# A gather ring with 24 more places, and a tile order of its own, for the last of four graph layers

## The chip, the cores and the metric

The kernel runs on one core of one Trainium2 chip. The metric is the device time of one execution in microseconds (us); less is better. The engines of the core are named as the profile names them: PE multiplies matrices, DVE works element by element, ACT evaluates functions, POOL (GpSimd) here mostly issues indirect DMAs and multiplies, and SP issues plain DMAs. PEld is PE's loading of weights.

## What is computed

Four layers of graph attention, each on a layer-normalised input and added to it. Eight batches of 2048 nodes with 64 features share one adjacency matrix, which is sparse: a node has about four neighbours on average, and the first ones have by far the most. The change concerns the fourth layer:

```python
def _layernorm(x, axis=-1, eps=1e-5):
    m = jnp.mean(x, axis=axis, keepdims=True)
    v = jnp.var(x, axis=axis, keepdims=True)
    return (x - m) / jnp.sqrt(v + eps)

def _L3_gnn_ref(x, adj, W, a):
    h = jnp.matmul(x, W)
    f1 = jnp.einsum('bnf,f->bn', h, a[:F_out, 0])
    f2 = jnp.einsum('bnf,f->bn', h, a[F_out:, 0])
    e = jax.nn.leaky_relu(f1[:, :, None] + f2[:, None, :], negative_slope=0.2)
    e = jnp.where(adj[None, :, :] > 0, e, NEG_BIG)
    attention = jax.nn.softmax(e, axis=2)
    return jax.nn.relu(jnp.matmul(attention, h))

# --- layer 3 (adj_preln) ---
h = jnp.maximum(_layernorm(x, axis=-1), 0.0)
x = x + _L3_gnn_ref(h, adj, L3_gnn_W, L3_gnn_a)
```

The other three layers are of the same kind: layer 1 has the same additive scores, layers 0 and 2 use dot products.

## The kernel before

**Tiles and slots.** The 2048 nodes are 16 tiles of 128, one node per partition; a row holds all eight batches, 512 features (`F`), and in the additive layers 8 further numbers (`B`), one score per batch. Each tile has a fixed number of slots, `ROWS[i]` plain ones and `PACKED[i]` packed ones: tile 0 has 9 + 8 = 17, tile 1 has 8, tile 2 has 6, tiles 3 to 5 have 5, tiles 6 to 10 have 4, and tiles 11 to 15 have 3; 81 in all. A slot is one gathered row for each of the 128 partitions. In a plain slot the neighbour belongs to the partition's own node. A packed slot holds the neighbours of nodes that have too many, and matrices of zeros and ones (`sel`, `selt`) carry values between node and slot through PE.

**The ring.** `gather` (L246) issues one indirect DMA on POOL for each slot of a tile, from the layer's table in HBM (2048 rows of 520 numbers) into the next place of `ring`, a buffer of `RING = 26` places. `held[i]` is the place at which tile i begins and `front` the next place to be filled. A place may be filled again only when the tile that was in it has been used up, in `weigh_sum`. The ring is shared by all layers.

**A layer as a pipeline.** `pipeline` (L214) takes stages and issues them in turn: in step n, each stage s works on the tile `order[n - s]`, the later stages first. What the engines run follows these program orders closely, though the framework may move an instruction by its own estimate of times. For layer 3, `additive(4, wd3, relu_add)` has these stages:

- `take` gathers the tile's rows.
- `sums` (L504) takes the exponentials of the rows' scores (ACT, L507) and adds them over a node's slots (`by_query`, PE, L399), for a bound of the softmax.
- `first` (L522) carries the node's own score to the packed slots (`by_edge`, PE, L412), adds, applies the leaky function, and takes the exponential (ACT, L542): the weights.
- `check` (L547) is `second`: sums of weights, and `weigh_sum` (L372), which multiplies two slots at a time by their weights on DVE (L380, `wg`) and adds them up in PSUM by a matmul with the identity or `selt` for each slot (PE, L385, `y`). After it the places of the tile are free. Beside it `xs_rows` loads the tile's `x` on SP (L259, six buffers).
- `third` (L553) divides on DVE (L465, `att`), transposes on PE (L306) and copies on ACT (L307, `xt`).
- `project` (L558) multiplies by the layer's matrix (PE, L561, `q`), and `relu_add` (L905) applies the relu, adds `x` on DVE (L906) and stores the result on SP (L907).

**What goes before.** The pipeline of layer 2's second half ends with `pre_d`, which computes the scores for layer 3 and stores `xh` into table 4; after the last tile it stores a mean row as well (`mr`, L366). Every gather of layer 3 needs the whole table, so layer 3 begins when that row has landed. Both pipelines take their working buffers from one pool, `rows2`, and use `ORDER`: tiles 13, 12, 11, 10, 9, 8, 0, 7, 6, 1, 5, 2, 4, 3, 14, 15.

Of the kernel before, what the change touches and what calls it, by code (L numbers as in the profile page):

```python
# [1 line left out]

# [6 lines left out]
F32 = mybir.dt.float32  # L9
# [7 lines left out]
P = 128  # L17
# [12 lines left out]
PACKED = [8, 2, 3, 3, 2, 1, 2, 1, 1, 1, 1, 2, 2, 1, 1, 1]  # L30
WIDTH = [128, 24, 24, 24] + [16] * 12
SEGS = [(24, 2), (16, 1)] + [(8, 1)] * 14
RING = 26
TEMP = 16.0

PAIRS = [0, 0, 2, 2, 2, 0, 0, 0, 2, 2, 2, 2, 2, 2, 2, 2]
# [4 lines left out]
ORDER1 = [13, 14, 15, 12, 11, 10, 0, 7, 6, 1, 5, 2, 4, 3, 9, 8]  # L41
ORDER2 = [8, 9, 10, 12, 11, 13, 0, 7, 6, 1, 5, 2, 4, 3, 14, 15]
ORDER = [13, 12, 11, 10, 9, 8, 0, 7, 6, 1, 5, 2, 4, 3, 14, 15]


def segments(n, count, least):
# [13 lines left out]
def edge_stack(ctx: ExitStack, tc: tile.TileContext, x_in, adj, w1, w1t, a1, wh, wht, bh, wo, bo,  # L60
# [10 lines left out]
    N, F = x_in.shape  # L71
    D = gamma.shape[0]
    B = F // D
# [3 lines left out]
    SLOTS = [k + t for k, t in zip(ROWS, PACKED)]  # L77
# [20 lines left out]
    most = const.tile([P, 5, NT], F32, name="most")  # L98
    least = const.tile([P, 2, NT], F32, name="least")
    ring = const.tile([P, RING, F + B], F32, name="g")  # L100
    qidx = const.tile([P, sum(PACKED)], I32, name="qidx")
# [5 lines left out]
    table = [tc.dram_tile([N + 2, F + B if k in (1, 4) else F], F32, name=f"table{k}")  # L107
             for k in range(5)]
# [9 lines left out]
    sel_all = [None]  # L118
# [93 lines left out]
    order = list(MAKING)  # L212
# [10 lines left out]
    bank, spot, rows_pool, more_pool, own_pool, thin = [None], [0], [None], [None], [None], [None]  # L223
# [7 lines left out]

    held, front = {}, [0]

    def rows(i, lo, hi, most=RING):

        t = lo
        while t < hi:
            at = (held[i] + t) % RING
            m = min(most, hi - t, RING - at)
            yield t, m, ring[:, at:at + m, :]  # L240
            t += m

    def row(i, t):
        return ring[:, (held[i] + t) % RING, :F]

    def gather(k, i, st):  # L246

        n = SLOTS[i]
        assert sum(SLOTS[j] for j in held) + n <= RING
        held[i], front[0] = front[0], (front[0] + n) % RING  # L250
        cols = table[k].shape[1]
        for t in range(n):
            nc.gpsimd.indirect_dma_start(  # L253
                out=ring[:, (held[i] + t) % RING, :cols], out_offset=None, in_=table[k][:, :],
                in_offset=bass.IndirectOffsetOnAxis(ap=idx[:, OFF[i] + t:OFF[i] + t + 1], axis=0))

    def load(st, name, src, bufs):
# [134 lines left out]
    def by_query(i, w, cols):  # L392


        K, T = ROWS[i], PACKED[i]
        w, packed = w if isinstance(w, list) else (w[:, :K, :], w[:, K:, :])
        p = (thin[0] or ps_m).tile([P, F], F32, name="m")
        for t in range(T):
            nc.tensor.matmul(p[:, :cols], selt(i, t), packed[:, t, :], start=(t == 0), stop=(t == T - 1))  # L399
        if K == 1:  # L400
            return w[:, 0, :], p[:, :cols]
        d = small.tile([P, cols], F32, name=f"row{cols}")
        nc.vector.tensor_reduce(d, w.rearrange("p k c -> p c k"), AX.X, OP.add)
        return d, p[:, :cols]
# [10 lines left out]
    def scores(i, st, q):  # L415

        K, s = ROWS[i], slots(s_all, i)
        qp = ps_q.tile([P, F], F32, name="q")
        nc.scalar.copy(qp, q)
        for t0, m, g in rows(i, 0, K, 2):  # L420
            pr = rows_pool[0].tile([P, 2, F], F32, name="prod")
            nc.vector.tensor_tensor(pr[:, :m], qp[:, None, :].to_broadcast([P, m, F]), g[:, :, :F],  # L422
                                    op=OP.mult)
            nc.vector.tensor_reduce(s[:, t0:t0 + m, :], pr[:, :m].rearrange("p t (b d) -> p t b d", b=B),
                                    AX.X, OP.add)
        for t in range(K, SLOTS[i]):
            qe = ps_q.tile([P, F], F32, name="q")
            nc.tensor.matmul(qe, sel(i, t - K), q, start=True, stop=True)  # L428
            pr = rows_pool[0].tile([P, 2, F], F32, name="prod")
            nc.vector.tensor_tensor(pr[:, 0], qe, row(i, t), op=OP.mult)  # L430
            nc.vector.tensor_reduce(s[:, t, :], heads(pr[:, 0]), AX.X, OP.add)
        return s
# [67 lines left out]
    def additive(k, wd, *finish):  # L500
# [213 lines left out]
    with tc.tile_pool(name="l2", bufs=2) as l2p, \  # L714
# [29 lines left out]
        def score(i, st, lo, hi):  # L744

            K, n = ROWS[i], hi - lo
            w = l2p.tile([P, max(ROWS), B * H], F32, name="w2", bufs=5)[:, :n]
            st.setdefault("w", []).append(w)
            s = ps_s.tile([P, F], F32, name="s2")[:, :n * B * H].rearrange("p (t c) -> p t c", c=B * H)
            for t in range(lo, hi):  # L750
                q = st["q"] if t < K else sent[i, t - K]
                g = ps_g.tile([P, F], F32, name="g2")
                nc.scalar.copy(g, row(i, t))  # L753
                pr = l2p.tile([P, B * H, D], F32, name="prod2")
                nc.vector.tensor_tensor(  # L755
                    pr.rearrange("p (b h) d -> p b h d", h=H),
                    q[:, :B * H * D].rearrange("p (b h d) -> p b h d", h=H, d=D),
                    heads(g)[:, :, None, :].to_broadcast([P, B, H, D]), op=OP.mult)
                nc.vector.tensor_reduce(s[:, t - lo, :], pr, AX.X, OP.add)  # L759
                nc.vector.tensor_tensor(s[:, t - lo, :], s[:, t - lo, :], q[:, B * H * D:], op=OP.subtract)  # L760
                nc.scalar.activation(w[:, t - lo], s[:, t - lo], AF.Exp, bias=mbb[:, OFF[i] + t:OFF[i] + t + 1])  # L761
                if t >= K:
                    fetch(stream.index((i, t - K)) + QE)
# [85 lines left out]
        thin[0] = None  # L849
    own.close()  # L850

    with psum_pools()[0] as ps_q, psum_pools()[1] as ps_t, tc.tile_pool(name="rows2", bufs=2) as rp:
        rows_pool[0] = rp
        order[:] = ORDER
        bank[0] = ps_t.tile([P, F], F32, name="tiny")
        sel_all[0] = rp.tile([P, sum(PACKED) * P], F32, name="sel", bufs=1)
        nc.sync.dma_start(out=sel_all[0], in_=sel_dram[:, :])

        def take3(i, st):
# [42 lines left out]
        pipeline(take3, first3, second3, third3, both(pre_b, xs_rows), fourth3, pre_b, pre_c(u3), pre_d(4, u3))  # L902


        def relu_add(i, st):  # L905
            nc.vector.scalar_tensor_tensor(st["x"], st["p"], 0.0, st["x"], op0=OP.max, op1=OP.add)  # L906
            nc.sync.dma_start(out=out[i * P:(i + 1) * P, :], in_=st["x"])  # L907

        additive(4, wd3, relu_add)


        nc.vector.memset(most[:, 3, :], 0.0)
# [527 lines left out]
```

## Time and profile before

| what | us |
|---|---|
| median of 3 runs | 1720.55 |
| lowest and highest | 1719.27, 1725.79 |
| the profiled execution | 1721.51 |
| its span, first to last instruction | 1719.7 |
| layer 3, from the issue of the mean row to the end | 1526.9 to 1719.7 |
| first and last gather of layer 3 begin | 1529.04 and 1670.20 |
| last store of layer 3 is issued | 1714.9 |

An instruction's row in the timeline gives its start and duration in us, the engine, the source line, the operation, the output and inputs by their names in the program, and in brackets how long the engine had been idle before it and what it then waited for. "issue" is a wait for nothing that the profile shows, and "remote" one for which it finds no source. Ends of matmuls are modelled. The view by stretches gives the busy time of each engine between two moments, then PE's granted clock as a share of the full one, the share of time in which the DMA engines were busy, and the bytes per second.

### The profile page before, as it was taken

To read this page: it belongs to the slowest core of one execution; us is meant where nothing else is said; L and a number is where in the kernel's file an instruction comes from. 1 tells how busy PE (TensorE), PEld (TensorE's weight loads), DVE (VectorE), ACT (ScalarE), POOL (GpSimd) and SP (SyncE) were. 2 spreads that over 40 slices of the span, in tenths; PEclk is the share of its full clock that TensorE was granted. 3 is DMA by queue.
4 is the path that set the end of the run, shared out by engine and by line. 5 is a ranking of instruction groups with operands and counts; after the bars stand their busy time and mean duration, and the time that the engine had idled before them with its cause. 6 is when DMAs were issued, how large, how long until landed. Compare 5 with 4: busy or idle time off the path is not lost.

```text
span 1719.7 us, 15784 instructions
## 1 busy us (share of the span) xinstructions
PE 1215.1 (71%) x3771; PEld 606.6 (35%) x3771; DVE 1318.4 (77%) x2748; ACT 744.5 (43%) x2378; POOL 1153.4 (67%) x903
## 2 busy tenths in 40 slices
PE   0025667776479974599997999999467877555877
PEld 0002334443234431234342444443223433333545
DVE  6979999992469987699997899831389889823656
ACT  5841324441146783356531545545234445620011
POOL 5766867786554125898789889985577896654540
PEclk9998876896699997799999999999787879657989
DMA  5555454455566447656255345200643542235651
GB/s 172 167 182 179 152 200 153 141 198 156 147 201 235 158 179 260 233 189 208 87 201 200 113 157 177 87 13 19 255 141 99 154 146 70 81 119 164 197 170 51
DMA packets 85787, 266.94 MB, mean 155 GB/s; under 512 B 14627, under 2 KB 14659, under 8 KB 75446
## 3 DMA queue, kind: packets, MB, share of 16 engines
q0 software_dynamic: 37328, 141.05, 26.7%
q1 hardware_dynamic: 48358, 124.79, 20.4%
q8 instruction: 32, 0.52, 0.1%
q14 instruction: 69, 0.57, 0.1%
HBM read 208.74 MB, written 57.05 MB: 155 GB/s over the span
## 4 chain that ended last, share of the span: by engine, by line
PE 25%; POOL 11%; DVE 9%; issue 7%; ACT 5%; DMA 3%; another core or an unknown queue 2%; DVEq 0%; SPq 0%; POOLq 0%; ACTq 0%
PE y L787 10%; PE y L385 4%; POOL g L253 3%; POOL wh L772 3%; PE m L836 2%; ACT yn L795 2%; PE m L824 2%; PE y L779 2%; POOL wg L380 1%; DMA g<-table,idx 1%; POOL ln_r L290 1%; DMA rows<-table 1%; PE m L399 1%; DVE prod L755 1%
## 5 line engine op out<-in xcount | busy, mean ns | idle before, releaser
L253 POOL DMA_INDIRECT g<-table,idx x405 | 399.2, 986 | 233.5 <-issue 161.7
L772 POOL TENSOR_TENSOR wh<-g,w 128x1024 f32<-128x1024 f32 x162 | 307.5, 1918 | 30.0 <-PE y L787 28.0
L385 PE MATMUL y<-wg,ident 128*128 128x512 f32 x392 | 234.5, 729 | 72.7 <-POOL wg L380 64.3
L290 POOL TENSOR_TENSOR ln_r<-ln_q,mhalf 128x8 f32<-128x8 f32 x80 | 135.8, 1701 | 160.6 <-DVE ln_q L288 85.1
L759 DVE TENSOR_REDUCE s<-prod 128x32 f32<-128x2048 f32 x81 | 184.0, 2286 | 14.8 <-ACT w L761 12.9
L380 POOL TENSOR_TENSOR wg<-g,w 128x1024 f32<-128x1024 f32 (+1 forms) x91 | 158.9, 1756 | 37.3 <-ACT w L436 24.2
L787 PE MATMUL y<-wh,ident 128*128 128x512 f32 x320 | 154.6, 610 | 28.9 <-POOL wh L785 25.1
L385 PE MATMUL y<-wg,selt 128*128 128x512 f32 x256 | 141.6, 663 | 5.4 <-POOL wg L380 4.4
L385 PEld LDWEIGHTS y<-wg,ident 128*128 128x128 f32 x392 | 81.6, 228 | 162.2 <-POOL wg L380 78.9
L787 PE MATMUL y<-wh,selt 128*128 128x512 f32 x256 | 124.7, 614 | 10.4 <-POOL wh L772 10.4
L795 ACT ACTIVATE yn<-y,rec 128x64 f32<-128x64 f32 x512 | 111.2, 368 | 27.5 <-PE y L787 26.9
L755 DVE TENSOR_TENSOR prod<-q,g 128x2048 f32<-128x2048 f32 x49 | 111.5, 2276 | 5.3 <-ACT g L753 4.6
L399 PE MATMUL m<-w,selt 128*128 128x8 f32 (+1 forms) x384 | 59.5, 258 | 76.0 <-ACT w L542 38.2
L380 DVE TENSOR_TENSOR wg<-g,tiny 128x1024 f32<-128x1024 f32 (+1 forms) x92 | 98.2, 1086 | 17.1 <-PE y L385 8.8
L399 PEld LDWEIGHTS m<-w,selt 128*128 128x128 f32 x384 | 63.5, 213 | 122.3 <-ACT w L542 43.6
L442 DVE SCALAR_TENSOR_TENSOR zt<-m,bhc,att 128x512 f32<-128x512 f32 x64 | 47.3, 738 | 75.0 <-ACT att L441 74.4
L298 ACT ACTIVATE xh<-x,ln_r 128x64 f32<-128x64 f32 x256 | 88.3, 428 | 18.8 <-POOL ln_r L292 18.7
L787 PEld LDWEIGHTS y<-wh,ident 128*128 128x128 f32 x320 | 59.0, 193 | 104.9 <-issue 63.8
L428 PE MATMUL q<-rows,sel 128*128 128x512 f32 x128 | 84.3, 762 | 15.7 <-DVE prod L422 5.0
L753 ACT COPY g<-g 128x512 f32<-128x512 f32 x81 | 50.4, 622 | 100.5 <-DVE prod L755 87.9
L755 DVE TENSOR_TENSOR prod<-qe,g 128x2048 f32<-128x2048 f32 x32 | 73.0, 2282 | 17.0 <-DMA qe<-qtab,qidx 15.9
L779 PE MATMUL y<-rows,ident 128*128 128x512 f32 x128 | 70.0, 634 | 18.3 <-DMA rows<-table 13.6
(210 smaller groups left out, 2584.7 us busy)
## 6 DMA issues: line engine op xcount, KB each, us to landing
qtab<-q SPq DMA_DIRECT2D x16, 1040.0 KB
a<-in_adj_dram SPq DMA_DIRECT2D x16, 1024.0 KB
q<-qtab SPq DMA_DIRECT2D x14, 1040.0 KB
table<-xh SPq DMA_DIRECT2D x48, 256.0 KB
rows<-table SPq DMA_DIRECT2D x48, 256.0 KB
xs<-x SPq DMA_DIRECT2D x48, 256.0 KB
x<-xs SPq DMA_DIRECT2D x48, 256.0 KB
table<-xh SPq DMA_DIRECT2D x32, 260.0 KB
```

The costliest lines, as they stand in the source:

```text
L253: nc.gpsimd.indirect_dma_start(out=ring[:, (held[i] + t) % RING, :cols], out_offset=None, in_=table[k][:, :], in_offset=bass.IndirectOffse ...
L290: nc.gpsimd.tensor_tensor(st["rstd"][:, 0, :], q, mhalf, op=OP.pow)
L298: nc.scalar.activation(dst[:, b * D:(b + 1) * D], st["src"][:, b * D:(b + 1) * D], func, bias=0.0 if st["less"] is None else r[:, 1, b:b + ...
L380: eng.tensor_tensor(wg[:, :m].rearrange("p t (b d) -> p t b d", b=B), g[:, :, :F].rearrange("p t (b d) -> p t b d", b=B), w[:, t0:t0 + m, ...
L385: nc.tensor.matmul(y, lhs(i, t), wg[:, t - t0, :], start=(t == 0 and own is None), stop=(t == n - 1))
L399: nc.tensor.matmul(p[:, :cols], selt(i, t), packed[:, t, :], start=(t == 0), stop=(t == T - 1))
L755: nc.vector.tensor_tensor(pr.rearrange("p (b h) d -> p b h d", h=H), q[:, :B * H * D].rearrange("p (b h d) -> p b h d", h=H, d=D), heads(g ...
L759: nc.vector.tensor_reduce(s[:, t - lo, :], pr, AX.X, OP.add)
L772: nc.gpsimd.tensor_tensor(wg, heads(row(i, t))[:, :, None, :].to_broadcast([P, B, 2, D]), w[:, :, 2 * k:2 * k + 2, None].to_broadcast([P, ...
L779: nc.tensor.matmul(st["ys"][j], ident, xb[:, 4 * j:4 * j + 4], start=True, stop=False)
L787: nc.tensor.matmul(st["ys"][j], lhs(i, t), wg[:, 4 * j:4 * j + 4], start=False, stop=(t == n - 1))
L795: nc.scalar.activation(yn[:, b, h, :], st["ys"][j][:, b, h, :], AF.Copy, scale=st["rec"][:, 4 * j + b, 2 * k + h:2 * k + h + 1])
```

## The change

Layer 3 gets a second ring buffer, `gmore`, of `MORE = 24` places behind the 26; `place` tells in which of the two a place lies, and `rows` cuts a tile where one ends. The fill point is set back to 0. The pool `rows2` is closed when layer 2's pipeline has been issued and a new one, `rows3`, is opened in its space, in which `gmore` is the first tile; `sel` moves to a pool `tail` around both. Layer 3 has its own order, `ORDER3`, in which tile 0 is ninth rather than seventh and tile 5 comes ahead of tile 1.

```diff
+MORE = 24
+ORDER3 = [13, 12, 11, 10, 9, 8, 7, 6, 0, 5, 1, 2, 4, 3, 14, 15]
@@ ring
+    rings, room = [ring], [RING]
+
+    def place(at):
+
+        return (rings[0], at, RING - at) if at < RING else (rings[1], at - RING, room[0] - at)
+
     def rows(i, lo, hi, most=RING):
 
         t = lo
         while t < hi:
-            at = (held[i] + t) % RING
-            m = min(most, hi - t, RING - at)
-            yield t, m, ring[:, at:at + m, :]
+            part, at, left = place((held[i] + t) % room[0])
+            m = min(most, hi - t, left)
+            yield t, m, part[:, at:at + m, :]
             t += m
@@ gather
-        assert sum(SLOTS[j] for j in held) + n <= RING
-        held[i], front[0] = front[0], (front[0] + n) % RING
+        assert sum(SLOTS[j] for j in held) + n <= room[0]
+        held[i], front[0] = front[0], (front[0] + n) % room[0]
         cols = table[k].shape[1]
         for t in range(n):
+            part, at, _ = place((held[i] + t) % room[0])
             nc.gpsimd.indirect_dma_start(
-                out=ring[:, (held[i] + t) % RING, :cols], out_offset=None, in_=table[k][:, :],
+                out=part[:, at, :cols], out_offset=None, in_=table[k][:, :],
@@ layer 2, second half, and layer 3
-    with psum_pools()[0] as ps_q, psum_pools()[1] as ps_t, tc.tile_pool(name="rows2", bufs=2) as rp:
-        rows_pool[0] = rp
+    with psum_pools()[0] as ps_q, psum_pools()[1] as ps_t, tc.tile_pool(name="tail", bufs=2) as tail:
+        layer = ExitStack()
+        rows_pool[0] = layer.enter_context(tc.tile_pool(name="rows2", bufs=2))
         order[:] = ORDER
         bank[0] = ps_t.tile([P, F], F32, name="tiny")
-        sel_all[0] = rp.tile([P, sum(PACKED) * P], F32, name="sel", bufs=1)
+        sel_all[0] = tail.tile([P, sum(PACKED) * P], F32, name="sel", bufs=1)
...
         pipeline(take3, first3, second3, third3, both(pre_b, xs_rows), fourth3, pre_b, pre_c(u3), pre_d(4, u3))
 
+        layer.close()
+        rows_pool[0] = layer.enter_context(tc.tile_pool(name="rows3", bufs=2))
+        order[:] = ORDER3
+        rings.append(rows_pool[0].tile([P, MORE, F + B], F32, name="gmore", bufs=1))
+        room[0], front[0] = RING + MORE, 0
...
         additive(4, wd3, relu_add)
+
+        layer.close()
```

More of the change, by code (lines that the diff above doesn't have):

```diff
@@ L1 @@
-from contextlib import ExitStack
+from contextlib import ExitStack, nullcontext
 import concourse.bass as bass
@@ L237, in rows @@
         while t < hi:
-            at = (held[i] + t) % RING
-            m = min(most, hi - t, RING - at)
-            yield t, m, ring[:, at:at + m, :]
+            part, at, left = place((held[i] + t) % room[0])
+            m = min(most, hi - t, left)
+            yield t, m, part[:, at:at + m, :]
             t += m
     def row(i, t):
-        return ring[:, (held[i] + t) % RING, :F]
+        part, at, _ = place((held[i] + t) % room[0])
+        return part[:, at, :F]
     def gather(k, i, st):
         n = SLOTS[i]
-        assert sum(SLOTS[j] for j in held) + n <= RING
-        held[i], front[0] = front[0], (front[0] + n) % RING
+        assert sum(SLOTS[j] for j in held) + n <= room[0]
+        held[i], front[0] = front[0], (front[0] + n) % room[0]
         cols = table[k].shape[1]
         for t in range(n):
+            part, at, _ = place((held[i] + t) % room[0])
             nc.gpsimd.indirect_dma_start(
-                out=ring[:, (held[i] + t) % RING, :cols], out_offset=None, in_=table[k][:, :],
+                out=part[:, at, :cols], out_offset=None, in_=table[k][:, :],
                 in_offset=bass.IndirectOffsetOnAxis(ap=idx[:, OFF[i] + t:OFF[i] + t + 1], axis=0))
```

## The prediction

> **What bounds the kernel now.** I read the page's head first, for the profiled execution itself.
>
> ```profile
> span 1719.7 us, 15784 instructions
> ```
>
> The execution took 1721.51 us, 1.8 us around its span and 0.96 us above the median of the runs, 1720.55 us. I add up on the span and then add 1.8 and take off 0.96.
>
> Next, the stretches of layer 3. It begins at 1526.9 us, when the mean row of its table is stored, and ends the kernel. I cut it where the timeline changes character.
>
> ```profile
> core 0: us, PE busy (x) PEld busy (x) DVE busy (x) ACT busy (x) POOL busy (x), PEclk, DMA share, GB/s
> 1527.00:1535.40 8.40, 0.00 (x0) 0.00 (x0) 0.00 (x0) 0.00 (x0) 4.84 (x5) 0.50 0.40 111
> 1535.40:1574.00 38.60, 17.39 (x50) 11.14 (x50) 9.93 (x45) 2.32 (x11) 25.60 (x27) 0.63 0.69 197
> 1574.00:1603.00 29.00, 23.20 (x102) 15.53 (x103) 19.56 (x82) 4.50 (x16) 10.44 (x11) 0.85 0.59 174
> 1603.00:1641.00 38.00, 29.05 (x109) 16.62 (x109) 19.56 (x59) 2.04 (x8) 19.90 (x21) 0.86 0.59 175
> 1641.00:1673.00 32.00, 28.31 (x108) 16.37 (x108) 21.66 (x74) 3.69 (x14) 16.11 (x17) 0.87 0.63 191
> 1673.00:1707.50 34.50, 32.91 (x165) 21.64 (x163) 28.55 (x108) 4.79 (x13) 0.00 (x0) 0.99 0.13 47
> 1707.50:1719.70 12.20, 4.84 (x20) 2.44 (x18) 3.45 (x9) 0.59 (x1) 0.00 (x0) 0.92 0.14 50
> ```
>
> PE carries most of the layer: 95% busy at clock 0.99 once the gathers are over (1673 to 1707.5), but 45% at clock 0.63 in the first 38.6 us. The question is what holds it there. The groups by line, in this window, show what the ring costs POOL:
>
> ```profile
> L253 POOL DMA_INDIRECT g<-table,idx x81 | 76.9, 949 | 71.6 <-issue 53.4 <-ACT xt L307 15.1 <-DVE tiny L529 0.6
> ```
>
> And POOL's timeline shows where:
>
> ```profile
> 1529.04 1.04 POOL L253 DMA_INDIRECT g<-table,idx  x1 [6.35 <-issue]
> ...
> 1568.00 0.94 POOL L253 DMA_INDIRECT g<-table,idx  x1 [0.30 <-issue]
> 1578.37 0.97 POOL L253 DMA_INDIRECT g<-table,idx  x1 [9.43 <-ACT xt L307]
> ...
> 1670.20 0.95 POOL L253 DMA_INDIRECT g<-table,idx  x1 [1.10 <-issue]
> ```
>
> Unhindered, gathers start every 1.253 us (1529.04 to 1568.00 for 31 steps). That is 32 gathers, then a wait: 26 places plus the 6 that tiles 13 and 12 gave back; the 33rd needs tile 11's. All 81 would take 80 x 1.253 + 0.95 = 101.2 us, to 1630.2; in fact the last ends at 1671.15. So 41 us of ring waits stand on POOL. They are not 41 us of the span: PE has rows queued for most of them. The full timeline shows what really stopped PE:
>
> ```profile
> 1557.35 0.59 ACT L307 COPY xt<-q 128x512 f32<-128x512 f32 x1 [8.00 <-issue]
> 1557.99 2.07 PE L561 MATMUL q<-wd,xt 128*128 128x128 f32 x8 [9.84 <-issue]
> 1563.27 2.34 PE L385 MATMUL y<-wg,selt 128*128 128x512 f32 x4
> 1573.45 0.69 DVE L906 SCALAR_TENSOR_TENSOR x<-q,x 128x512 f32<-128x512 f32 x1 [13.32 <-remote]
> 1574.27 0.60 PE L399 MATMUL m<-w,selt 128*128 128x8 f32 x2 [8.66 <-DVE rec L459]
> ```
>
> DVE's L906 needs tile 13's projection, which PE shows ended at 1560.06, yet it starts at 1573.45, 4.5 us after POOL's last gather of the run. ACT's L307 needs transposes that PE shows ended at 1548.1. PE's completions reach the others 9 and 13 us late while gathers stream. Layer 1 does the same in its run of 35 gathers:
>
> ```profile
> 445.20 0.95 POOL L253 DMA_INDIRECT g<-table,idx  x1 [0.30 <-issue]
> 434.30 0.17 DVE L535 TENSOR_TENSOR s<-g,m 128x16 f32<-128x16 f32 x1 [8.21 <-remote]
> 451.10 0.60 ACT L570 ACTIVATE e<-q 128x512 f32<-128x512 f32 x1 [29.48 <-remote]
> ```
>
> ACT waits 29.5 us and goes on 4.95 us after the gathers stop at 446.15. Twice, then, PE worked normally for some 18 us of a stream and was released fully only when it broke. The ring's fullness is what breaks it.
>
> **What the Trainium skill says.** "Perfetto Trace Analysis", Tensor Engine Instruction: PE's end is estimated, and the semaphore goes out only when PSUM acknowledges. So a shown end is not a release; the 13.3 us agree. "SBUF — State Buffer", Who interferes with whom: DMA never contends with a compute engine. The trace doesn't bear this out for gathers from POOL. "TensorE: Matmul & The Clock Gate", What's actually happening: an idle PE falls to half clock; here 0.63 in the starved stretch against 0.99.
>
> **The change part by part.**
>
> 1. The ring has 50 places. Slots in the new order: 3, 3, 3, 4, 4, 4, 4, 4, 17, 5, 8, 6, 5, 5, 3, 3. The first six tiles are the same as before, so until 1566 everything runs as before. With tiles 13 and 12 returned, 56 gathers go out without a break; the 57th needs tile 11. The run ends at 1529.04 + 56 x 1.253 = 1599.2 instead of 1569.
>
> 2. If PE is held to the end of the run, it resumes 4.5 us later, at 1603.7, where it resumed at 1574: 30 us lost. What it has still to do is the same: busy time times clock of the stages from 1574 on is 19.7 + 25.0 + 24.6 + 32.6 + 4.5 = 106.4 us at full clock. With all rows there, it goes at 95%: 112 us. Add 3.5 us for a cold start (the half clock from 1574 to 1581 now), 1.9 us for the last tile's own chain (6.7 us, of which PE 4.84) and 5.5 us from the last matmul to the end: 1603.7 + 122.9 = 1726.6. Before, the same work took 140.2 us to 1714.2, 34 us above the work, from idle time and half clock; 23 us of that is won, and 30 lost.
>
> 3. PE may be let through once in the longer run, as at 1557. It does then some 8 us at half clock, 4 us of work, but returns a tile of 3 or 4 places, which lengthens the run by 4 to 5 us. I take 0; bounds -5 and +5.
>
> 4. The other 25 gathers follow as places come free, 3 to 5 at a time. Runs that short held nothing before (1642 to 1671); runs of 17 cost 7.9 us of PE idle at 1634 and 1641. I take +1; bounds 0 and +16.
>
> 5. Tile 0 ninth: its 17 rows arrive while PE has 29 others, so PE never runs dry on data. Hidden by point 2, since PE is held anyway; worth more only without the hold.
>
> 6. Closing the pool of rows before layer 3: up to six loads of `x` (256 KB each), issued before 1517 now, must wait until the old tiles are free, and share SP's queue and the DMA engines with the last `xh` and mean rows. A megabyte and a half at the 260 KB/us that the trace shows at 1575 is 6 us. `x` is first needed at 1573, so I take 0; if they go ahead of the mean row the gathers start up to 5 us later.
>
> 7. `sel` moves pool and `gmore` takes other rows' space: first needed at 1561, long free. Splits of a tile at a ring's end: one fell in tiles 9 and 4 before, one in 6 and 14 now; 46 multiplications either way (35 + 11 shown). Nothing.
>
> Sum: 1726.6 + 1 = 1727.6 on the span against 1719.7; with 1.8 - 0.96, 1728 us. That is +0.4%, inside the 0.5% that a measurement of this kernel can tell from no change.
>
> **Rivals.**
>
> A. The hold has its length in itself (8 and 16 us in both runs) and does not wait for the stream's end. For: both first releases came in mid-stream (434.3, 1557.4). Against: both last ones came 4.5 and 4.95 us after it. Then PE starts at 1535.4, does 117.4 us of work at 95% (123.6), loses the 18.5 us of its two stalls, 7 us of half clock and 7 later, with 7.4 at the end: 1699 on the span, 1700 in time; 1685 to 1712.
>
> B. No hold: the waits were a product of the full ring. Without the 25 us: 1674. Against: PE stopped at 1549 while the ring still took gathers.
>
> C. Slower: the hold returns after 1604, because POOL, always with places to fill, never pauses for 3 us. Place: the 25 last gathers; price: twice the 7.9 us of the 17-gather run, 1743. It decides if more than some 15 gathers follow on one another after the release.
>
> D. PE's work sets the layer and nothing moves: 1718. Against: of the 192.7 us, 117.4 are PE work.
>
> **How the numbers follow.** Forecast 0.44 (own range 1716 to 1738), A 0.27, B 0.12, C 0.12, D 0.05. Faster by over 0.5% (below 1712): A, B and 0.02 of the forecast, 0.41. Slower (above 1729): C and 0.21 of it, 0.33. The same: the rest, 0.26. The range leaves out most of B and half of C: 1682 to 1742. It is wide since cases of both signs stand in it.
>
> **What would show it.** POOL's gathers in one run of about 56 to some 1599, then a pause; an all-engine stall that ends 4 to 5 us after; waits marked remote of over 20 us on DVE or ACT; then PE at 95%. PE at work between 1575 and 1600 proves me wrong and A or B right; two or more remote waits after 1605 speak for C; a first gather later than 1530 for point 6.

## The result, and the profile after

The changed kernel takes 1744.79 us (median of 4 runs, 1740.81 to 1747.86), the kernel before beside it 1722.87 us (4 runs, 1719.27 to 1725.79). The ratio is 1.0128, with a 95% interval from 1.0105 to 1.0151: 1.3% slower. The forecast was 1728 us. The profiled execution is the one of 1747.86 us; its page begins:

```profile
span 1746.0 us, 15789 instructions
```

That is 26.3 us more than the span before. The stretches of layer 3, cut where its character changes (us, then busy time and count of each engine, TensorE's clock, DMA share, GB/s):

```profile
1530.00:1541.80 11.80, 0.00 (x0) 0.00 (x0) 0.00 (x0) 0.03 (x1) 7.68 (x8) 0.50 0.78 259
1541.80:1608.20 66.40, 18.77 (x50) 11.39 (x50) 9.54 (x45) 2.49 (x11) 45.53 (x48) 0.55 0.70 202
1608.20:1645.00 36.80, 28.36 (x113) 18.05 (x114) 26.12 (x102) 5.21 (x19) 14.23 (x15) 0.85 0.54 162
1645.00:1685.00 40.00, 35.77 (x146) 21.93 (x145) 23.19 (x72) 4.08 (x16) 9.48 (x10) 0.87 0.42 124
1685.00:1705.00 20.00, 19.07 (x86) 11.59 (x85) 16.34 (x55) 2.35 (x8) 0.00 (x0) 1.00 0.16 52
```

The second row holds the loss. In 66.4 us PE makes 50 matmuls; before, the stretch in which it made its first 50 was 38.6 us long. The work is the same, and the 28 us between the two go by while POOL issues gathers. The timeline shows how (start, length, engine and line, and the idle time ahead with what ended it; the rows between are left out):

```profile
1531.13 2.71 SPq L269 DMA_DIRECT2D x<-xs  x6
1531.88 1.04 POOL L263 DMA_INDIRECT g<-table,idx  x1 [6.22 <-DMA table<-mr]
1541.77 0.22 ACT L517 ACTIVATE w<-g 128x24 f32<-128x24 f32 x1 [14.19 <-DMA g<-table,idx]
1559.92 1.11 PE L316 MATMUL q<-ident,att 128*128 128x128 f32 x4 [4.40 <-remote]
1566.91 0.17 DVE L545 TENSOR_TENSOR s<-g,m 128x16 f32<-128x16 f32 x1 [9.79 <-issue]
1578.11 0.17 DVE L520 TENSOR_TENSOR S<-m,w 128x8 f32<-128x8 f32 x1 [11.03 <-issue]
1589.35 0.59 ACT L317 COPY xt<-q 128x512 f32<-128x512 f32 x1 [22.07 <-issue]
...
1600.90 0.95 POOL L263 DMA_INDIRECT g<-table,idx  x1 [0.31 <-issue]
1608.21 0.69 DVE L923 SCALAR_TENSOR_TENSOR x<-q,x 128x512 f32<-128x512 f32 x1 [16.08 <-remote]
1610.33 0.17 DVE L469 TENSOR_TENSOR rec<-m,w 128x8 f32<-128x8 f32 x1 [1.42 <-remote]
1614.66 0.97 POOL L263 DMA_INDIRECT g<-table,idx  x1 [12.81 <-ACT xt L317]
```

From 1531.88 to 1601.85 there are 69.97 us, 56 gathers at 1.25 us, then POOL waits 12.8 us: the run that the prediction's first point worked out. ACT's L317 and DVE's L923 wait 22 and 16 us for PE, and DVE goes on 6.4 us after the last gather of the run; a second release follows at 1610.33, 8.5 us after it.

PE's completions are not all held until then. DVE's L545 and L520 and ACT's L317 read what PE shows ended at 1555.1, 1555.5 and 1561.0, and go on in the middle of the run, at 1566.91, 1578.11 and 1589.35: one at a time, 11.2 us apart. Two other runs of 56 gathers below have the same spacing (1561.67, 1572.87, 1584.12 with the ring alone; 1562.08, 1573.27, 1584.52 with the late plain loads). So a long run lets single completions through, late, and the rest come after its end.

What those 66 us cost PE stands in the waits of that window (engine, line, what it waited for; total us, times, longest):

```profile
PEld q L571 <- issue: 29.4, 1, 29.4
PE q L571 <- issue: 29.0, 1, 29.0
ACT xt L317 <- issue: 22.1, 1, 22.1
```

One wait of 29 us in front of the projection L571. It is listed as "issue", but L571 reads the `xt` that ACT copies, and ACT stood at L317 for the transposes' release.

After the release PE needs 132.5 us (1608.2 to its last matmul's end at 1740.7); before it needed 140.7 (1573.45 to 1714.16). So the 26.3 us are: 2.8 from a later first gather (1531.88 against 1529.04), 30.1 from 24 more gathers at 1.253, 1.9 from a longer way from the run's end to the release (6.4 against 4.5), less 8.5 from the release to the end of the span (137.8 against 146.25). The 2.8 are no part of the change that I can name: the first gather stands at 1526.7 with the ring alone and at 1535.0 with the late plain loads, and neither run changes anything ahead of it.

### The profile page after: what moved, and what is told of

The parts are those of the page before. It is cut to its first block, busy times and chain, and to the rows that moved or that the text cites. A ratio compares the mean times of both kernels' runs of the same rounds, so it can differ in the third digit from the quotient of the medians.

```text
span 1746.0 us, 15789 instructions
## 1 busy us (share of the span) xinstructions
PE 1225.1 (70%) x3771; PEld 611.2 (35%) x3771; DVE 1323.5 (76%) x2747; ACT 745.9 (43%) x2378; POOL 1153.8 (66%) x903
## 3 DMA queue, kind: packets, MB, share of 16 engines
q0 software_dynamic: 37328, 141.05, 26.3%
## 4 chain that ended last, share of the span: by engine, by line
PE 26%; POOL 11%; DVE 10%; issue 8%; ACT 5%; another core or an unknown queue 1%; DMA 1%; POOLq 0%; DVEq 0%; ACTq 0%; SPq 0%
PE y L797 10%; PE y L395 5%; POOL g L263 4%; POOL wh L782 3%; PE m L846 2%; ACT yn L805 2%; PE m L834 2%; PE y L789 2%; POOL ln_r L300 1%; DVE prod L432 1%; POOL wg L390 1%; PE m L409 1%; DVE prod L765 1%; PE q L571 1%
## 5 line engine op out<-in xcount | busy, mean ns | idle before, releaser
L263 POOL DMA_INDIRECT g<-table,idx x376 | 371.1, 987 | 204.9 <-issue 131.1
L395 PE MATMUL y<-wg,ident 128*128 128x512 f32 x392 | 245.4, 758 | 72.7 <-POOL wg L390 58.4
L769 DVE TENSOR_REDUCE s<-prod 128x32 f32<-128x2048 f32 x81 | 184.0, 2286 | 14.7 <-ACT w L771 12.8
L805 ACT ACTIVATE yn<-y,rec 128x64 f32<-128x64 f32 x512 | 111.2, 367 | 28.3 <-PE y L797 27.7
L409 PE MATMUL m<-w,selt 128*128 128x8 f32 (+1 forms) x384 | 60.1, 259 | 82.2 <-ACT w L552 38.6
L438 PE MATMUL q<-rows,sel 128*128 128x512 f32 x128 | 84.8, 768 | 14.1 <-DVE x L483 4.5
L390 DVE TENSOR_TENSOR wg<-g,tiny 128x1024 f32<-128x1024 f32 (+1 forms) x76 | 80.6, 1079 | 11.8 <-PE y L395 5.1
L317 ACT COPY xt<-q 128x512 f32<-128x512 f32 x80 | 46.2, 581 | 89.9 <-PE q L316 53.5
```

What stands on the lines that cost most here:

```text
L263: nc.gpsimd.indirect_dma_start(out=part[:, at, :cols], out_offset=None, in_=table[k][:, :], in_offset=bass.IndirectOffsetOnAxis(ap=idx[:, ...
L390: eng.tensor_tensor(wg[:, :m].rearrange("p t (b d) -> p t b d", b=B), g[:, :, :F].rearrange("p t (b d) -> p t b d", b=B), w[:, t0:t0 + m, ...
L395: nc.tensor.matmul(y, lhs(i, t), wg[:, t - t0, :], start=(t == 0 and own is None), stop=(t == n - 1))
L805: nc.scalar.activation(yn[:, b, h, :], st["ys"][j][:, b, h, :], AF.Copy, scale=st["rec"][:, 4 * j + b, 2 * k + h:2 * k + h + 1])
```

## The experiments

H is the theory of the prediction: a run of gathers holds back PE's completions until it ends, so a ring that lengthens the run costs what it lengthens (the single ones above aside). O is that the order does it; F that the edits have a fixed price; others are named in the expectations.

The runs fell on at least five chips, and this matters more than anything else below. On two of them, which I call chips with the hold, the kernel before takes 1721 to 1725 us; on three others, without it, 1673 to 1674. Each ratio is against runs of the kernel before on the same chip, so ratios are compared, and times only within a group. On which chip the kernels before and after of the first section ran isn't recorded; by time and trace it has the hold.

### The parts of the change, with the hold

**The ring alone** (the order of before is kept):

```diff
-        order[:] = ORDER3
+        order[:] = ORDER
```

> The changed kernel with the old tile order in layer 3: the 24 places and the new pool alone. Theory H: first run 56 gathers, release some 76 us after the first gather, 1738 to 1750 us like the changed kernel. Rival O: the order is put back, 1718 to 1728 us.

Measured: 1739.99 us (4 runs) beside 1721.29, ratio 1.0103, interval 1.0047 to 1.0159. 56 gathers again, to 1596.6; DVE's L923 is released at 1602.97 after 16.07 us. The ring alone is enough. The order's own share can't be told from nothing, since the two intervals overlap. The reverse, the new order without more places, can't be built: tiles 0, 5 and 1 stand together in it and need 17 + 5 + 8 = 30 of 26 places. So there is no result for the order alone.

**A dose between**: 10 more places in place of 24.

```diff
-MORE = 24
+MORE = 10
```

> The changed kernel with 10 more places instead of 24. On a chip with the hold: theory H a ratio of 1.004 to 1.010, a first run of 42 gathers and a release 5 to 6 us after its end; a fixed price of the edits 1.011 to 1.015. On a chip without it 1.002 to 1.004, as three times before.

Measured: 1733.78 us (19 runs) beside 1725.49, ratio 1.0040, interval 1.0025 to 1.0055. The end of the run and the release in its timeline:

```profile
1584.50 0.95 POOL L263 DMA_INDIRECT g<-table,idx  x1 [0.30 <-issue]
1591.11 0.59 ACT L317 COPY xt<-q 128x512 f32<-128x512 f32 x1 [19.98 <-remote]
...
1594.03 0.95 POOL L263 DMA_INDIRECT g<-table,idx  x1 [8.59 <-issue]
```

The run has 39 gathers, from 1536.8 to 1585.4, and not 42: only one of the first two tiles had been given back. The release is 5.7 us after its end; here it frees ACT's L317, which in the runs of 56 passed in mid-run, 11.2 us after the one before it; here it comes 9.1 us after (1581.97), so by this row alone it stands only some 2 us apart from that spacing. So with 32, 39 and 56 gathers in the run, release follows first gather by 44.4, 54.3 and 76.3 us: the release moves with the run's end. The time lies at the lower edge of what H expected, and little above what the same kernel costs without the hold (below): the dose shows in the timeline and not clearly in the time.

The way from the run's end to the release isn't fixed either. It is 2.1 us after a run of 12 (in the paused run below, where DVE goes on at 1567.12 after a run that ended at 1565.00), 4.5 after 32, 4.95 after layer 1's 35, 5.7 after 39, and 8.5 after 56 if the second release is taken, which the ring alone (8.5) and the late plain loads (8.3) repeat. It grows with the run. Why, no run here shows.

### Is it the gathers?

**Plain loads from SP.** Each gather of layer 3 becomes a plain transfer of the tile's own 128 rows; layer 3 so works on each node's own row in place of its neighbours' rows.

```diff
+            if k == 4:
+                nc.sync.dma_start(out=part[:, at, :cols], in_=table[k][i * P:(i + 1) * P, :cols])
+                continue
             nc.gpsimd.indirect_dma_start(
                 out=part[:, at, :cols], out_offset=None, in_=table[k][:, :],
```

> The changed kernel; each gather of layer 3 is replaced by a plain DMA from SP of the same 128 rows of 520 numbers, taken in order from the tile's own rows rather than by index, so layer 3's result is another one. Bytes, places, waits and everything on PE, DVE and ACT stay. Theory H in its narrow form (it is POOL's gathers that hold PE back): no hold, PE works from its first rows on, 1670 to 1705 us. Rival D (any dense stream of DMA writes into SBUF holds PE back): waits of over 8 us remain and the time is 1730 us or more.

> The same plain transfers issued by SP. On a chip with the hold: 0.969, as before. On a chip without it: if the gap between the kernel before and the run with POOL's plain transfers (18 us) is the pace of the gathers and not POOL as issuer, the same as POOL's, a ratio of 0.985 to 0.993.

Measured, both with the hold: 1670.97 us, ratio 0.9688 (0.9633 to 0.9743), and 1671.76 us, ratio 0.9704 (0.9669 to 0.9739).

**Plain loads from POOL**: the same, with `nc.gpsimd.dma_start`.

> The changed kernel with plain transfers of the tile's own 128 rows issued by POOL in place of layer 3's gathers (each node's own row stands in for its neighbours'). On a chip with the hold (before near 1720): theory P (POOL's issuing holds PE) a ratio of 0.988 to 1.013 with waits of over 8 us on ACT or DVE; theory I (the scattered addressing does) 0.968 to 0.975 as with loads from SP. On a chip without it: 0.989, as twice before.

Measured, with the hold: 1677.71 us beside 1725.02, ratio 0.9729 (0.9695 to 0.9764). Its layer 3 by windows, at the time of its 55 loads:

```profile
1537.00:1560.00 23.00, 18.65 (x83) 12.03 (x84) 15.80 (x76) 3.47 (x12) 15.54 (x29) 0.85 0.98 366
1560.00:1580.00 20.00, 17.80 (x78) 10.85 (x77) 17.56 (x62) 3.12 (x12) 8.54 (x16) 1.00 0.98 360
1580.00:1600.00 20.00, 19.27 (x111) 15.48 (x110) 14.04 (x57) 3.56 (x11) 5.32 (x10) 0.88 0.67 212
```

And its timeline in layer 1, where the gathers were left as they are:

```profile
453.50 0.60 ACT L583 ACTIVATE e<-q 128x512 f32<-128x512 f32 x1 [30.83 <-remote]
```

One execution, both pictures. Layer 1's gathers hold ACT for 30.8 us; in layer 3 no wait from 1537 to 1600 is marked remote, the longest that ACT has for PE is 4.0 us, and PE is busy four fifths of the time and more while the DMA engines are at 98% until 1580, denser than the 70% of the gathers. So neither dense writing nor POOL as issuer is enough for the hold; of what was run, only the indirect transfers have it. The Trainium skill ("DMA: Bandwidth & Descriptors", Terms) says that transfers of the software kind have their descriptors written to rings in SBUF, while the hardware kind feeds them to the DMA engines directly. In the trace of this run, the queue of POOL's plain loads is of the software kind, as the gathers' is:

```profile
q0 software_dynamic: 4400, 14.65, 25.2%
```

So software descriptors alone don't make the hold.

Two things limit this. A plain load of a tile's own rows waits for no other tile, so 26 of the 81 went out in layer 2, from 1427 on: part of the gain is an earlier start. And POOL's plain loads come with more gaps than gathers (mostly 0.3 to 0.9 us, for landings or places, though from 1537 to 1570 they still start more often than gathers do). What the earlier start and the pace are worth by themselves shows without the hold:

> The changed kernel with every gather of layer 3 replaced by a plain transfer of the tile's own 128 rows that POOL still issues (as in the run with plain loads from SP; layer 3 so works on each node's own row in place of its neighbours' rows, the amount of work is the same). Theory P (the hold belongs to transfers that POOL issues, scattered or not): PE's completions are held again while the stream runs, at least one wait of over 8 us on ACT or DVE between 1545 and 1610, and 1700 to 1745 us. Theory I (the hold belongs to the scattered, row by row addressing): none, PE near full clock from 1560, 1665 to 1680 us as with loads from SP.

> The changed kernel with plain transfers of the tile's own 128 rows, issued by POOL, in place of layer 3's gathers (each node's own row stands in for its neighbours'; the amount of work is the same). On a chip with the hold (before near 1720): theory P (transfers that POOL issues hold PE's completions) 1700 to 1745 us with waits of over 8 us on ACT or DVE; theory I (the scattered addressing does) 1665 to 1680 us, as with loads from SP. On a chip without it: 1650 to 1658 us, as in the run before, and nothing told apart.

1654.13 and 1654.77 us beside 1673.48 and 1673.23, ratio 0.9888 both times (0.9858 to 0.9918, 0.9868 to 0.9908): 19 us without any hold. With it the same kernel gains 47 us. The other 28 us are an estimate, the difference of the two, of what the hold costs the kernel before in layer 3.

### Without the hold

**The changed kernel itself**, on such a chip:

> The changed kernel once more, beside the others on one chip. The four runs before this fell on a chip on which the kernel before takes 1673 us, and on which the traces show no completion of PE that is late by more than 1 us in the first runs of gathers. If this is such a chip again (before near 1673), theory H (the change's loss is the hold times the longer run) gives a ratio of 0.99 to 1.003; theory F (a fixed price in the edits) 1.01 to 1.015. If it is a chip with the hold (before near 1720): 1.010 to 1.015 by both.

Measured: 1676.26 us (6 runs) beside 1673.23, ratio 1.0021, interval 1.0002 to 1.0040. POOL's first and last gathers in its timeline:

```profile
1502.74 1.04 POOL L263 DMA_INDIRECT g<-table,idx  x1 [6.23 <-DMA table<-mr]
...
1602.87 0.95 POOL L263 DMA_INDIRECT gmore<-table,idx  x1 [0.30 <-issue]
```

and the windows beside them:

```profile
1512.10:1545.00 32.90, 24.38 (x90) 16.29 (x91) 18.23 (x86) 5.03 (x20) 24.98 (x27) 0.69 0.80 237
1545.00:1580.00 35.00, 29.26 (x131) 18.65 (x130) 24.43 (x93) 4.65 (x16) 26.47 (x29) 0.90 0.87 269
1580.00:1603.00 23.00, 22.27 (x92) 12.93 (x91) 16.52 (x45) 2.22 (x8) 17.21 (x20) 1.00 0.89 283
```

All 81 gathers in one run of 101 us with no wait for a place, since places come back in time; and PE works through it, 90 matmuls in the first row against 50 in twice that time above. No wait in it is marked remote. So the longest run of all is harmless here, and of the loss of 1.3% some 0.2% are left. F, a fixed price of 1%, falls. In this trace every one of PE's completions is recorded 0.01 to 0.88 us after the end that the profile shows. The prediction read its 13.3 us as the way from a shown end to a release; that way is short, and the 13.3 us are the hold.

**10 more places**, three times:

> The changed kernel with 10 more places instead of 24. Theory H (the hold ends when the first run of gathers ends): 36 places and the 6 that come back give a first run of 42, which ends near 1584.5 on the span; release 5 to 6 us later, near 1590; from the release to the end between the 145.7 us of the kernel before and the 137.8 us of the changed one, 142: 1732 on the span, 1734 us (1729 to 1739). Theory F (the loss is a fixed price of the edits, order, pools or splits, and not of the length of the run): 1741 to 1748, as with 24 more.

> The changed kernel with 10 more places instead of 24. On a chip with the hold: theory H 1729 to 1739 us (a ratio of 1.004 to 1.010), with a first run of 42 gathers and the release 5 to 6 us after its end; theory F as the changed kernel, 1741 to 1748. On a chip without it 1676 to 1682 us, as before.

> The changed kernel with 10 more places instead of 24. On a chip with the hold: theory H 1729 to 1739 us beside a before of 1722, a ratio of 1.004 to 1.010, a first run of 42 gathers and a release 5 to 6 us after its end; a fixed price of the edits 1.011 to 1.015. On a chip without it 1.002 to 1.004, as before.

All three fell on chips without the hold, so they don't part H from F. Ratios 1.0041 (1.0027 to 1.0054), 1.0026 (1.0007 to 1.0045) and 1.0031 (1.0019 to 1.0043). A slightly negative worth of the ring is real, since all three intervals lie above 1: one tenth to four tenths of a percent, and I can't say from what. With the hold the same kernel had 1.0040: the hold's own share of that dose is within the spread.

**The closed pool of rows alone** (no added places, old order; six loads of `x` wait for it):

```diff
-        order[:] = ORDER3
-        rings.append(rows_pool[0].tile([P, MORE, F + B], F32, name="gmore", bufs=1))
-        room[0], front[0] = RING + MORE, 0
+        order[:] = ORDER
```

> The changed kernel without the added places and with the old order: what is left is the closing of the pool of rows ahead of layer 3, which holds back six loads of x. In the changed kernel the first multiplication on gathered rows came 6.4 us later than before (3.0 at the mean row, 3.5 at the landing). If the closed pool makes that, and it is on the path: 1726 to 1731 us. If those 6 us are hidden by the hold or came from elsewhere: 1720 to 1724 us.

1675.89 us (20 runs) beside 1673.48, ratio 1.0006, interval 0.9995 to 1.0017: nothing that can be told from no change, as the prediction had it. The two ranges expected are for a chip with the hold and don't apply.

This kernel is the nearest to the kernel before that has a trace without the hold, and shows where the two kinds of chip part. Its profiled execution has a span of 1679.6 us, 40.1 less than the kernel before. From layer 1's first gather to layer 2's it takes 235.8 us against 257.1, and from layer 3's first gather to the end 168.0 against 190.65: these two layers make up the whole difference.

### Breaking the run

**A pause after every 12 gathers.** POOL reads the last gathered row, so it waits until that has landed, and then raises one 128x8 to a power. In the changed kernel (the lines left out make each later gather follow the pause):

```diff
...
+            sent_rows[0] += 1
+            if k == 4 and sent_rows[0] % 12 == 0:
+                junk = small.tile([P, B], F32, name="junk8")
+                pause[0] = nc.gpsimd.tensor_tensor(junk, one8, part[:, at, F:], op=OP.mult).ins
+                with tc.issue_after(pause[0]):
+                    pause[0] = nc.gpsimd.tensor_tensor(junk, one8, mhalf, op=OP.pow).ins
```

> The changed kernel; after every 12 gathers of layer 3 POOL waits for the last one's rows to land and then does one power of 128x8 (1.70 us in this kernel) before it goes on. Six pauses of about 5 us, so POOL needs 131 us instead of 101 for its 81 gathers. Theory H: PE's completions come through in each pause, no wait marked remote of over 8 us in layer 3; PE has 117 us of work and starts 10 us into the layer; 1685 to 1712 us. Rival S (PE is late because its rows or its own order of work are late, the run of gathers is incidental): POOL's 30 us more cannot help, 1740 to 1775 us.

Measured, with the hold: 1721.03 us (20 runs) beside 1721.29, ratio 0.9994 (0.9979 to 1.0010). Outside both ranges expected: the change's loss is gone, which S excluded, and no gain over the kernel before came, which H forecast. In its timeline, two pauses and what PE's readers wait around them:

```profile
1548.04 0.20 POOL L274 TENSOR_TENSOR junk<-one,g 128x8 f32<-128x8 f32 x1 [2.96 <-DMA g<-table,idx]
1548.31 1.68 POOL L276 TENSOR_TENSOR junk<-one,mhalf 128x8 f32<-128x8 f32 x1
...
1567.24 0.59 ACT L328 COPY xt<-q 128x512 f32<-128x512 f32 x1 [5.68 <-remote]
1568.12 0.20 POOL L274 TENSOR_TENSOR junk<-one,g 128x8 f32<-128x8 f32 x1 [3.12 <-DMA g<-table,idx]
```

The 22 and 16 us are gone, a 5.7 us wait is left inside a run of 12, and each pause costs POOL some 5 us, so that its last gather ends at 1664.

The same pauses in the kernel before, in layers 1 and 3:

> The kernel before with its 26 places and its order; in layers 1 and 3 POOL waits after every 12 gathers until the last has landed, and raises one 128x8 to a power. On a chip with the hold the stalls of layer 1 (8.2, 16.1 and 3.1 us) and of layer 3 (6.7, 7.8, 5.0) should shrink to half or less. Theory H: 15 to 30 us faster, 1690 to 1706, a ratio of 0.983 to 0.991. Rival: the gathers, which end 20 us or more later with the pauses, become the bound: 1.00 or over. On a chip without the hold: only the pauses' price, 1.000 to 1.015.

> The kernel before with a pause after every 12 gathers in layers 1 and 3. On a chip without the hold it cost 1.9%. On a chip with it theory H expects the stalls of 27 us in layer 1 and 20 us in layer 3 to shrink to half, less the 1.9%: a ratio of 0.99 to 1.01. If the pauses do not break the hold, 1.015 or over.

The first fell on a chip without the hold: 1703.47 us beside 1673.23, ratio 1.0192 (1.0166 to 1.0219), the bare price of the pauses, and more than the 1.015 expected at most. The second fell on one with it: 1711.04 us (6 runs) beside 1725.02, ratio 0.9921 (0.9896 to 0.9946). The same edit loses 30 us on one chip and wins 14 on another: what it frees of the hold is worth some 44 us, an estimate that takes its price for the same on both. Where the hold is, this version beats the kernel before by 0.8%; elsewhere none that computes the same beats it. Nothing here does so on all chips.

### What follows the release

The forecast failed most after the release: 117.4 us, and 1 for short groups, against 132.5. Two runs ask whether the 25 gathers left by then make it.

**Pauses among the 25 only**, after every 4 (`sent_rows[0] > 56` in the condition):

> The changed kernel; only after the first 56 gathers of layer 3, POOL waits after every 4 gathers until the last has landed and then raises one 128x8 to a power (1.7 us). The first run and its release at about 1608 stay. After the release PE had 106.3 us of work at full clock and took 132.2 us. Theory L (short holds by the 25 late gathers make most of the excess): it takes 120 to 126 us, 1731 to 1738 us in all. Theory W (the excess is the cold start, rows that come late and the tiles' own dependencies): nothing won, 1742 to 1750 us.

It fell on a chip without the hold, so it has no release: 1684.69 us beside 1673.48, ratio 1.0073 (1.0039 to 1.0107). By the ratios, from two chips, the pauses cost half a percent on top of the change's 1.0021, and nothing is told of L or W.

**The 25 as plain loads from SP**; for these rows each node's own row stands in for its neighbour's.

```diff
...
+            sent_rows[0] = sent_rows[0] + 1 if len(held) > 1 or t else 1
+            if k == 4 and sent_rows[0] > 56:
+                nc.sync.dma_start(out=part[:, at, :cols], in_=table[k][i * P:(i + 1) * P, :cols])
+                continue
```

> The changed kernel; of layer 3's 81 gathers the first 56 stay, and the 25 others are plain transfers of the tile's own 128 rows from SP (for these rows each node's own row stands in for its neighbour's; the amount of work is the same). On a chip with the hold (before near 1722) the first run and its release stay. Theory L (the 25 late gathers make the excess over the forecast after the release): from the release to PE's last matmul 115 to 121 us in place of 132, 1728 to 1735 us, a ratio of 1.003 to 1.008. Theory W (cold start and the tiles' own dependencies): 129 to 135 us and a ratio of 1.010 to 1.016. On a chip without the hold (before near 1673): 0.994 to 1.001.

Without the hold: 1674.98 us beside 1674.24, ratio 0.9996 (0.9979 to 1.0013). The changed kernel has 1.0021 (1.0002 to 1.0040) there, so some 4 us may come from the plain loads without any hold; the two intervals overlap.

> The changed kernel; the first 56 gathers of layer 3 stay, the 25 others are plain transfers of the tile's own 128 rows from SP (for these rows each node's own row stands in for its neighbour's). On a chip with the hold (before near 1722): theory L (the 25 late gathers make the excess over the forecast after the release) 115 to 121 us from the release to PE's last matmul in place of 132, 1728 to 1735 us, a ratio of 1.003 to 1.008; theory W (cold start and the tiles' own dependencies) 129 to 135 us, 1.010 to 1.016. On a chip without the hold: 0.998 to 1.001, as in the run before.

With it: 1746.00 us (4 runs) beside 1725.49, ratio 1.0114 (1.0090 to 1.0139). By the total, L is wrong, and from the first release to PE's last matmul's end it takes 128.2 us, between L's range and W's. Its windows after the release say more:

```profile
1625.00:1645.00 20.00, 17.55 (x79) 11.15 (x80) 17.16 (x63) 2.85 (x12) 0.00 (x0) 1.00 0.71 215
1645.00:1665.00 20.00, 19.27 (x114) 14.46 (x113) 15.21 (x59) 3.86 (x15) 0.00 (x0) 0.95 0.61 197
1665.00:1685.00 20.00, 19.23 (x60) 9.59 (x59) 14.20 (x30) 1.24 (x4) 0.00 (x0) 0.97 0.15 54
```

and so do the two releases in its timeline:

```profile
1604.01 0.95 POOL L267 DMA_INDIRECT g<-table,idx  x1 [0.30 <-issue]
1606.20 0.69 DVE L927 SCALAR_TENSOR_TENSOR x<-q,x 128x512 f32<-128x512 f32 x1 [18.90 <-remote]
...
1613.21 0.17 DVE L473 TENSOR_TENSOR rec<-m,w 128x8 f32<-128x8 f32 x1 [6.32 <-remote]
```

From the second release to PE's last matmul's end it takes 121.2 us (1613.2 to 1734.4); in the changed kernel 130.4 (1610.3 to 1740.7). The clock is 0.95 to 1.00 from 1625 on. From the first gather to the second release the two take the same, 78.2 and 78.5 us. So the stretch in which the 25 are plain loads is 9 us shorter. Of this the span keeps 3.2 (1742.8 against 1746.0): the layer began 3.1 us later, and the end after PE's last matmul took 8.4 us in place of 5.3. That longer end belongs to the edit, since the same kernel without the hold has it too (8.5, against 5.6 in the changed kernel there). The ratio, 1.0114 against 1.0128, tells no gain from none. That the late gathers cost some 9 us therefore rests on one execution with the hold, and how much of it is hold and how much the pace of the rows stays open.

## Why the prediction was right or wrong

**Point 1, right.** A run of 56, to 1599.2 forecast; 1601.85 measured, from a start 2.8 us later.

**Point 2, the hold: right in the main on this chip, but not of every chip.** The release came 6.4 us after the run's end, and a second at 8.5, and not 4.5: the way grows with the run, where the prediction took it as fixed. The runs with 39 and 56 gathers, the pauses and the plain loads all bear out that most completions come after the run's end; three single ones came before it. What no line of the profile before could show is that it is a matter of the chip.

**Point 2, the work left: right.** 106.4 us at full clock forecast, 106.6 from PE's busy time and its clock after the release.

**Point 2, "With all rows there, it goes at 95%": the step that failed.** The forecast was 112 us, 3.5 for the cold start and 1.9 for the last tile, 117.4; measured 132.5. Of the 23 us to be won back, 8.2 came. The rate is right where its condition holds: counted back from the last matmul over 106.3 us of PE work at full clock, the kernel with SP's plain loads takes 115.2 us, 8.9 of them idle and none lost to half clock. The changed kernel, counted so, takes 128.7, with 13.6 idle and 8.7 lost to half clock; with the ring alone it is 124.3. All rows were not there: 25 gathers still came in short groups until 1670. Of the clock's loss after the release, 3.9 us lie in the cold start, which the forecast had at 3.5, and 5.1 in two later falls to half clock, at 1656.8 and 1667.1, for which it had nothing. I had looked at the 24 gathers that the longer ring brings ahead and not at the 25 that it leaves behind. With these 25 as plain loads 9 us of the excess went; what makes the rest is not shown.

**Point 3, right within its bounds.** PE got new work in the run at 1559.92, where it had waited for DVE's `att`, ended at 1557.1, and at 1589.99, once `xt` was copied. It gave back no tile that lengthened the run.

**Point 4, mis-sized.** +1 taken, of bounds 0 to +16; some 9 by the one execution with the late plain loads. It is the same miss as above, seen from the gathers. Small holds returned: waits of PE of 2.1 and 3.5 us at 1634.8 and 1652.8, about the runs of 8 and 7 gathers. That is rival C's mechanism at a third of its price, 5.6 us of 15.8.

**Points 5 and 7**: nothing to be seen of either; the run with the ring alone shows the order too small to tell.

**Point 6, right to take 0.** The six loads of `x` went out with the first gathers, at 1531.1. The first exponential of gathered rows (ACT, L517) came 9.9 us after the first gather and not 6.4 as before. These 3.5 us lie inside the run, whose end sets the release, so they don't show; without the hold the closed pool costs 0.06%, nothing that can be told.

The sum of the misses: 2.7 at the end of the run (the later start), 1.9 at the release, 14.1 after it against 118.4, less 0.2 at the end make 18.4 after rounding, which is the 1746.0 of the span less the forecast's 1727.6.

**The rivals.** A is right in part, since single completions come in mid-run, 11.2 us apart; its 1700 falls with the hold, where the release follows the run. B falls there as well; that its 1674 is the time of the chips without the hold is luck, since on the others the waits were no product of the full ring. C's 1743 lies next to the 1744.79 measured, and remote waits after 1605 were its sign (1608.21 and 1610.33 are the release itself; ACT has one of 5.9 us until 1655.64); but the run of over 15 late gathers that it asked for didn't come, the longest has 8, and its small holds cost a third of its price. So its number, too, is luck for the most part. D's picture, that the ring's waits lie beside PE's own work and nothing moves, is nearly what the chips without the hold show: 0.2% for the change on one of them. The prediction gave it 5 in 100, since the trace it was read from has the hold.

**Open.** What in an indirect transfer holds PE's completions, and why only on some chips. The traces with the hold lack records. In the kernel before, 1075 updates of PE's semaphore stand for 1151 instructions that raise it, 1209 of 1297 for ACT and 2192 of 2432 for DVE; on the chips without the hold none is missing. They are missing where gathers run: in the changed kernel from 1541.8 to 1608.15, 1 of 14 of PE's is there, 1 of 11 of ACT's and 8 of 37 of DVE's; where POOL's plain loads took the gathers' place, all are there. So the hold and the loss of records go together, and the loss isn't PE's alone. Every run here is recorded, so it isn't excluded that the recording takes part in the hold; no run here tries it.

## What to carry to other kernels

A buffer that lets one engine run further ahead is worth something only if its wait was on the path; first ask what that wait was giving others in the meantime. When a forecast says "then everything is there and PE runs at its rate", count what is still to be issued at that moment. And a stall that no dependency explains should be looked at on a second chip before a kernel is tuned to it: the pauses that win 0.8% on one lose 1.9% on another.

## What the runs showed of the hardware

The same program takes 1721 to 1725 us on some chips and 1673 to 1674 on others, 3% apart. The difference lies in two layers with long runs of POOL's indirect gathers, and on the first kind of chip PE's completions reach ACT and DVE late there: up to 28.3 us after the shown end in layer 3 of the changed kernel, 29.6 in layer 1 of the run with POOL's plain loads (423.88 to 453.50). In a run of 56 single ones come every 11.2 us, most in a burst after the run, 4.5 us after 32 gathers and 8.3 to 8.5 after 56. DVE's own reach PE at most 2.8 us late in the changed kernel's run (1557.11 to 1559.92). Plain transfers, whether from SP or POOL, do not do it on the same chip at 360 GB/s and more. The Trainium skill ("SBUF — State Buffer", Who interferes with whom) says that DMA never contends with a compute engine. The plain loads and the chips without the hold agree. Inside a held run the instructions themselves are no longer either: ACT's copy takes 0.59 us at 1589.35 in the run and at 1613.97 after it. What comes late is the word that they are done, and no run here shows a contention in SBUF behind it.
